# Sorted edge sources placed by one-hot matrix products in PSUM instead of by indirect sends to memory

## The chip, the cores and the metric

The kernel runs on one core of one Trainium2 chip. The metric is the device time of one execution in microseconds; of several executions the median is taken. The profile is one further execution, taken by the hardware profiler.

## The reference

The reference computes one layer of a graph network over 3125 nodes with 256 channels. A normalised copy `xn` of the input goes through two branches whose results are added to the input: a message-passing network (103,125 edges sorted by target, each message a gathered node row and 64 edge attributes, summed by target, followed by a small dense network), and four layers of linear attention with a feed-forward part. Then comes a mixture of four experts, whose gates come from a graph attention over 65,536 unsorted edges. This last part matters here:

```python
h = (x_flat @ W_gat).reshape(M, HEADS, NUM_EXPERTS)
...
a_src = (h * att_src).sum(-1)
a_dst = (h * att_dst).sum(-1)
e = jax.nn.leaky_relu(a_src[src] + a_dst[dst], negative_slope=0.2)
e_max = jax.ops.segment_max(e, dst, num_segments=M)
ee = jnp.exp(e - e_max[dst])
denom = jax.ops.segment_sum(ee, dst, num_segments=M)
alpha = ee / (denom[dst] + 1e-16)
msg = h[src] * alpha[:, :, None]
agg = jax.ops.segment_sum(msg, dst, num_segments=M)
```

To sum by target, the kernel sorts the edges by target itself: it needs, for each place in the sorted order, the source node of the edge that belongs there. Edges whose target is past the last of the 3125 nodes do not count.

## The kernel before

Nodes lie in 25 tiles of 128. The program is one stream of Python code that deals instructions to the engines; a scheduler keeps each engine's queue in order. The parts are these.

**Messages.** `gather_chunk` fetches one row per partition for 806 columns by indirect transfers from GpSimd's queue (line 456), and `sum_up` (line 468, VectorE) adds along the columns. The sums are stored in `run_d`.

**Attention and feed-forward.** The loop over `DEPTH` = 4 layers is TensorE's main work. Between its pieces, calls of `pace(us)` and `beside(us)` deal out other work. `clock["now"]` is a planned time; `pace` advances it, and lets columns of the messages, pieces of the node network and sends follow when their planned time has come. `beside` takes jobs from a list: counting (`count_group`), range tables (`ends_tile`), and 64 placement groups (`place_group`).

**Placement.** The 65,536 edges lie as 128 partitions by `TE` = 512 columns. `place_group` handles 8 columns: with one-hot products it finds each edge's rank in the sorted order (`number`). After four groups `laid` turns 32 columns of ranks into addresses `place`: rank r belongs to partition r // tv, column r % tv of the sorted layout, where tv is 400, or 512 when the edges are many.

**Sends.** `send(t)` (line 736) issues one indirect transfer from GpSimd's queue that writes 128 sources, one of 4 bytes per partition, to their addresses in the memory buffer `by_dst`; 512 of them in all. They begin when the last message column is summed, one per 1.38 us of the planned clock, and no sooner than their place is known. `by_dst` is first filled with a node `NONE` that stands for "no edge"; its row of the table carries a score of -1e30. `sorted_edges` loads the sorted sources `si` back once all sends have landed (line 881).

**Node network.** `message_nodes` starts when the messages are done. `fetch` (line 534) gathers the sums of two tiles by indirect transfers into `aggr` (three buffers), `pair` (lines 539 to 608) runs the small dense network on them in some fifteen pieces. A fetch stands in GpSimd's queue behind the sends that were issued before it.

**Edges.** After the last layer's feed-forward, `finish` (lines 780 to 816) adds the branches, computes the 24 numbers of each node, writes them to the table `tab_d` and to the target positions `tgt_d`. Then 400 indirect gathers by the columns of `si` (line 1064) bring the table's rows, `edge_chunk` runs the softmax along them, and the four experts are computed beside. The last part joins partitions, gates and writes out.

Other lines that the text names: line 643 `one_hot`, line 686 `ohT` (VectorE's comparisons of the placement), lines 695, 722 and 723 its scan and reduction, lines 706 to 720 its products, lines 1011 and 1024 the two products of the feed-forward, line 1021 its 16-bit bias product of 512 columns, line 544 the two-scalar comparison `goes_on`, line 1056 the first row that the edge stage gathers.

Of the kernel before, what the change touches and what calls it, by code (L numbers as in the profile page):

```python
# [48 lines left out]
FEW = 400  # L49
NONE = NT * P - 1  # L50
FF2 = 512
# [6 lines left out]
def kernel(ctx: ExitStack, tc: tile.TileContext, a: dict, out: bass.AP):  # L58
# [131 lines left out]
    tab = state.tile([P, NT, ROW + 1], F32, name="tab")  # L190
    tab_d = dram.tile([NP, ROW], F32, name="tab_d")
    gx_d = dram.tile([NP, D], F32, name="gx_d")
# [120 lines left out]

    pairs0 = so.tile([P, TE], I32, name="pairs0", tag="pairs")
    lo = so.tile([P, TE], F16, name="lo")
    hi = so.tile([P, TE], F16, name="hi")
    row_h = dram.tile([TE // GC, GC * P], F16, name="row_h")
    with tc.tile_pool(name="tmp", bufs=1) as tmp:
# [16 lines left out]
        V.tensor_copy(lo, d)  # L335
        V.tensor_scalar(pairs0, e_src, float(N - 1), None, op0=ALU.min)
    bins = const.tile([P, P, GC], F16, name="bins")
    G.iota(bins, pattern=[[1, P], [0, GC]], base=0, channel_multiplier=0, allow_small_or_imprecise_dtypes=True)
# [59 lines left out]
    def ends_sum():  # L398
# [3 lines left out]
        nc.sync.dma_start(f0[0:P - 1, 1:2], f0[1:P, 0:1])  # L402
        V.tensor_scalar(d0, f0[:, 0:1], 0.0, float(N - 1), op0=ALU.max, op1=ALU.min)
        G.iota(first_t, pattern=[[P, NT]], base=0, channel_multiplier=0, allow_small_or_imprecise_dtypes=True)
# [45 lines left out]
    def gather_chunk():  # L450
        t0 = STARTS[len(chunks)]
        k = min(KM, TM - t0)
        m = mg.tile([P, KM, DM], F32, name="m_run", bufs=3)
        attributes(m, t0, k)
        for t in range(k):
            last_gather[0] = G.indirect_dma_start(  # L456
                out=m[:, t, :D], out_offset=None, in_=xn_d,
                in_offset=bass.IndirectOffsetOnAxis(ap=src_i[:, t0 + t:t0 + t + 1], axis=0))
        chunks.append(m)
# [18 lines left out]

    last_gather = [None]
    for _ in range(3):  # L480
# [6 lines left out]

    pieces = []

    def piece():  # L490
# [4 lines left out]
    def pace(us):  # L495
# [13 lines left out]
        while (clock["columns"] == TM and clock["sent"] < clock["placed"]  # L509
               and FIRST + COLUMN * (TM + NT + clock["sent"] - 32) <= clock["now"]):  # L510
            send(clock["sent"])
            clock["sent"] += 1


    def message_nodes():
        mi_open.close()
        pw = early.enter_context(tc.tile_pool(name="pw", bufs=1))
        wk2 = early.enter_context(tc.tile_pool(name="wk2", bufs=1))
# [12 lines left out]
        def fetch(c):  # L531
            agg = wk2.tile([P, 2, DM], F32, name="aggr", bufs=3)
            for i, t in enumerate(c):
                last_gather[0] = G.indirect_dma_start(  # L534
                    out=agg[:, i, :], out_offset=None, in_=run_d,
                    in_offset=bass.IndirectOffsetOnAxis(ap=sum_i[:, t:t + 1], axis=0))
            fetched[c[0]] = agg

        def pair(c):
            agg = fetched[c[0]]  # L540
            k, n0, w = len(c), c[0] * P, len(c) * P
            for i, t in enumerate(c):
                goes_on = wk2.tile([P, P], F32, name="goes_on")
                V.tensor_scalar(goes_on, ids, last_t[:, t:t + 1], cont, op0=ALU.is_equal, op1=ALU.mult)
                ps = pg.tile([P, DM], F32, name="ps_g")
                T.matmul(ps, goes_on, last_m, start=True, stop=True)
                V.scalar_tensor_tensor(agg[:, i, :], agg[:, i, :], has_m[:, t:t + 1], ps, op0=ALU.mult, op1=ALU.add)
                yield False
            xr = wk2.tile([P, 2, D], F32, name="xr", bufs=2)
            nc.sync.dma_start(xr[:, :k, :], xn_d[n0:n0 + w, :].rearrange("(c p) d -> p c d", p=P))  # L550
            h0 = wk2.tile([P, 2, D], F32, name="h0", bufs=2)
            cmv = small.tile([P, 4, 2], F32, name="cmv")
# [43 lines left out]
            yield False  # L596
            xin = wk2.tile([P, 2, D], F32, name="xin")
            if c[-1] < NT - 1:
# [9 lines left out]
            nc.sync.dma_start(gx_d[n0:n0 + w, :].rearrange("(c p) d -> p c d", p=P), h0[:, :k, :])  # L608
            if c[0] + 6 < NT:
                fetch(PAIRS[c[0] // 2 + 3])  # L610

        for c in PAIRS[:3]:
            fetch(c)
        pieces.extend(pair(c) for c in PAIRS)

    place = so.tile([P, TE], I32, name="place")
    tv = state.tile([P, 1], F32, name="tv")
    many_i = state.tile([P, 1], I32, name="many_i")
    tv_less, tv_inv, tv_gap = (state.tile([P, 1], F32, name=f"tv_{k}") for k in range(3))

    def laid(dst, r):

# [5 lines left out]
        V.tensor_scalar(a, rem, tv, None, op0=ALU.is_ge)  # L628
        V.scalar_tensor_tensor(a, rem, 0.0, a, op0=ALU.is_lt, op1=ALU.subtract)
        V.tensor_tensor(a, q0, a, op=ALU.subtract)  # L630
        V.tensor_scalar(a, a, float(P), tv_gap, op0=ALU.min, op1=ALU.mult)
        V.tensor_tensor(dst, a, r, op=ALU.add)
    by_dst = dram.tile([2 * E2, 1], I32, name="by_dst")
    by_p = by_dst[:E2, :].rearrange("(p t) o -> p (t o)", t=TE)
    nothing = so.tile([P, TE], I32, name="nothing", tag="hr", bufs=2)
    V.memset(nothing, NONE)
    nc.sync.dma_start(by_p, nothing)
    start_d = dram.tile([P, LO], F32, name="start_d")
# [40 lines left out]
    def place_group(t):  # L679
# [31 lines left out]
        if late:  # L711
# [12 lines left out]
            if (t + GC) % SG == 0:  # L724
                laid(place[:, t + GC - SG:t + GC], number[t // SG % 2])
                clock["placed"] = t + GC
# [5 lines left out]

    def send(t):

        with tc.issue_after(last_gather[0].ins):
            i = G.indirect_dma_start(out=by_dst, out_offset=bass.IndirectOffsetOnAxis(ap=place[:, t:t + 1], axis=0),  # L736
                                     in_=pairs0[:, t:t + 1], in_offset=None)
        tc.declare_no_dep(i.ins, group="by_dst", reason="each place is written once")
        tc.add_to_no_dep_group("by_dst", i.ins)

# [39 lines left out]
    def finish(c):  # L780
# [22 lines left out]
        for i in range(2):  # L803
# [4 lines left out]
                            prod[:, :k, :].rearrange("p t (h e) -> p t h e", h=H4), AX.X, ALU.add)  # L808
        if c[-1] == NT - 1:
            V.tensor_scalar(tab[:, NT - 1, HG:HG + H4], tab[:, NT - 1, HG:HG + H4], no_node, None, op0=ALU.add)  # L810
        nc.sync.dma_start(tab_d[n0:n0 + w, :].rearrange("(c p) f -> p c f", p=P), tab[:, c[0]:c[-1] + 1, :ROW])

# [20 lines left out]
    for p0 in range(0, P, 32):  # L833
        nc.sync.dma_start(by_edge[p0:p0 + 32, FEW:, :].rearrange("p t f -> p (t f)").rearrange("p (a b) -> p a b", b=128),
                          zeros[p0:p0 + 32, :, :128].to_broadcast([32, (TE - FEW) * ROW // 128, 128]))
    no_node = state.tile([P, 1], F32, name="no_node")
    V.tensor_scalar(no_node, bin_p, LAST - 0.5, -BIG, op0=ALU.is_ge, op1=ALU.mult)
    V.memset(tab[:, :, ROW:], 1.0)
# [4 lines left out]
    def edge_ranges():  # L843
# [30 lines left out]
        V.tensor_tensor(start_i, start, away, op=ALU.add)  # L874

    edges = {}

    def sorted_edges():

        si = so.tile([P, TE], I32, name="si", tag="oh_hi", bufs=2)  # L880
        tc.keep_in_program_order(nc.sync.dma_start(si, by_p))
        edges.update(si=si)

# [155 lines left out]
    while clock["sent"] < TE:  # L1039
        pace(COLUMN)  # L1040
    sorted_edges()
    early.close()
# [15 lines left out]
    tgt_p = tgt_d[:E2, :].rearrange("(p t) h -> p t h", t=TE)  # L1058
    si = edges["si"]

# [339 lines left out]
```

## Time and profile before

| what | us |
|---|---|
| median of 3 runs (2829.52 to 2834.2) | 2831.46 |
| the profiled execution | 3944.21 |
| its span, first to last instruction | 3942.5 |
| TensorE busy with products | 2327.2 |
| GpSimd busy | 1782.9 |
| VectorE busy | 1440.1 |
| ScalarE busy | 991.9 |
| 806 message gathers on GpSimd, 996 ns each | 802.5 |
| 512 sends on GpSimd, 969 ns each | 495.9 |
| 400 edge gathers on GpSimd, 954 ns each | 381.4 |

The mean granted TensorE clock in it is 0.765. The profiled execution is 1113 us longer than the median run. Durations of single instructions are read from it; how long the engines stand idle between them is not the same in the other runs. A row of a group gives its line, engine, operation, tiles, shape and count, then busy us and the mean ns of one, then the idle time ahead of it and what ended it ("issue": nothing that the profile shows; "remote": another engine that it does not name). PE is TensorE, PEld its weight loads, DVE VectorE, ACT ScalarE, POOL GpSimd, SP the engine that issues the plain transfers.

### The profile page before, as it was taken

The page shows a single profiled execution, that of the slowest core. Times are in us where ns is not written, and L with a number is a line of the kernel's source. Part 1 is how long each engine was busy: PE and PEld are TensorE (multiplying, and loading weights), DVE is VectorE, ACT ScalarE, POOL GpSimd, SP SyncE. Part 2 cuts the span into 40 slices and gives each one's busy share as a digit, 9 for nine tenths or more (in the row PEclk, how much of TensorE's full clock was granted, in tenths as well). Part 3 has the DMA queues.
Part 4 walks back from the last instruction along what each step waited for, and adds up shares of the span by engine and source line. Part 5 has one row for each costly group of instructions (what it writes and reads, how often), then busy time and mean ns, then how long its engine had stood idle before and what let it go on. Part 6 is the DMA issues. An engine that isn't in the chain of part 4 may idle for free. (4 is left out here: it accounts for less than half of the span.)

```text
span 3942.5 us, 33476 instructions
## 1 busy us (share of the span) xinstructions
PE 2327.2 (59%) x11139; PEld 1603.3 (41%) x11139; DVE 1440.1 (37%) x4221; ACT 991.9 (25%) x1721; POOL 1782.9 (45%) x1843
## 2 busy tenths in 40 slices
PE   1756466566488765834563556448268746657471
PEld 1544343445255552523352445336245523334241
DVE  4645354464534544312232333324201112121227
ACT  2312123241122411211221332214123312122121
POOL 3446544454635546365435333430630355554634
PEclk9877687788699977966776777768578867777675
DMA  8446555664645646400001101001000111110101
GB/s 245 151 143 220 178 158 150 188 213 142 207 150 188 227 131 199 145 18 17 26 25 28 49 20 35 18 11 32 16 7 14 22 15 30 12 30 15 26 14 35
DMA packets 282448, 350.07 MB, mean 89 GB/s; under 512 B 180015, under 2 KB 229686, under 8 KB 269462
## 3 DMA queue, kind: packets, MB, share of 16 engines
q1 hardware_dynamic: 211558, 232.39, 18.4%
q0 software_dynamic: 70704, 115.42, 11.2%
q8 instruction: 90, 1.47, 0.2%
q14 instruction: 96, 0.79, 0.1%
HBM read 193.09 MB, written 154.56 MB: 88 GB/s over the span
## 5 line engine op out<-in xcount | busy, mean ns | idle before, releaser
L456 POOL DMA_INDIRECT m_run<-xn_d,src_i x806 | 802.5, 996 | 828.1 <-issue 230.1
L736 POOL DMA_INDIRECT by_dst<-pairs,place x512 | 495.9, 969 | 329.1 <-DVE near L657 161.7
L1064 POOL DMA_INDIRECT rows_c<-tab_d,si x400 | 381.4, 954 | 300.1 <-DVE rows_c L1120 181.2
L468 DVE SCALAR_TENSOR_TENSOR m_run<-m_run,stay 128x320 f32<-128x320 f32 x805 | 439.6, 546 | 98.4 <-DMA m_run<-xn_d,src_i 50.9
L1011 PE MATMUL ps_a<-hT,w 128*128 128x512 f32 (+1 forms) x896 | 405.4, 609 | 80.6 <-ACT hT L164 44.6
L1024 PE MATMUL ps_a<-w,gT 128*128 128x256 f32 x1600 | 380.9, 390 | 58.5 <-issue 57.8
L1024 PEld LDWEIGHTS ps_a<-w,gT 128*128 128x128 f32 x1600 | 310.3, 195 | 122.2 <-issue 80.3
L1152 PE MATMUL ps_a<-hT,we 128*128 128x512 f32 (+1 forms) x448 | 233.5, 654 | 150.5 <-issue 98.6
L1011 PEld LDWEIGHTS ps_a<-hT,w 128*128 128x128 f32 x896 | 177.0, 214 | 283.2 <-issue 178.8
L1163 PE MATMUL ps_t<-we,hf 128*128 128x256 f32 x800 | 201.3, 404 | 83.3 <-issue 61.5
L1027 DVE TENSOR_TENSOR xm<-ps_a,xm 128x512 f32<-128x512 f32 (+1 forms) x52 | 34.9, 670 | 522.8 <-remote 266.5
L1152 PEld LDWEIGHTS ps_a<-hT,we 128*128 128x128 f32 x448 | 92.5, 219 | 305.4 <-issue 241.6
L534 POOL DMA_INDIRECT aggr<-run_d,sum_i x25 | 24.6, 983 | 414.2 <-PE ps_t L557 387.2
L1163 PEld LDWEIGHTS ps_t<-we,hf 128*128 128x128 f32 x800 | 159.9, 203 | 127.8 <-issue 80.6
L1014 ACT ACTIVATE gT<-ps_a,b 128x512 f32<-128x512 f32 (+1 forms) x224 | 142.8, 641 | 239.7 <-PE ps_a L1011 157.5
L581 PE MATMUL ps_a<-gh,gw 128*128 128x256 f32 (+1 forms) x312 | 99.1, 464 | 165.1 <-issue 99.2
L709 ACT ACTIVATE earlier<-ps_t 128x512 f16<-128x512 f32 x128 | 71.8, 594 | 397.0 <-PE ps_t L708 179.1
L695 DVE TENSOR_TENSOR_SCAN run<-goes,ps_g 128x288 f16<-128x288 f16 x64 | 48.1, 751 | 322.6 <-remote 184.0
L994 PE MATMUL ps_a<-co,qT 128*128 128x256 f32 x400 | 123.1, 459 | 72.2 <-ACT qT L953 38.1
L581 PEld LDWEIGHTS ps_a<-gh,gw 128*128 128x128 f32 x312 | 67.8, 235 | 187.3 <-issue 107.7
L971 PE MATMUL ps_g<-vk 128*128 128x128 f32 x400 | 80.0, 330 | 101.7 <-ACT vk L969 60.3
L159 PE MATMUL ps_t<-ident,hn 128*128 128x128 f32 x450 | 90.5, 335 | 69.2 <-ACT hn L122 28.2
(375 smaller groups left out, 3803.5 us busy)
## 6 DMA issues: line engine op xcount, KB each, us to landing
run_d<-m_run SPq DMA_DIRECT2D x100, 1280.0 KB
m_run<-in_edge_attr_dram SPq DMA_DIRECT2D x95, 256.0 KB
hr<-row_h SPq DMA_DIRECT2D x64, 256.0 KB
m_run<-xn_d,src_i POOLq DMA_INDIRECT x806
w<-in_L_mix_W_dram SPq DMA_DIRECT2D x8, 1024.0 KB
by_dst<-pairs,place POOLq DMA_INDIRECT x512
rows_c<-tab_d,si POOLq DMA_INDIRECT x400
run_d<-rows_c SPq DMA_DIRECT2D x16, 300.0 KB
```

The costliest lines, as they stand in the source:

```text
L159: T.transpose(ps[:, i * P:(i + 1) * P], src[:, c * P:(c + 1) * P], ident)
L456: last_gather[0] = G.indirect_dma_start(out=m[:, t, :D], out_offset=None, in_=xn_d, in_offset=bass.IndirectOffsetOnAxis(ap=src_i[:, t0 + t ...
L468: add = V.scalar_tensor_tensor(m[:, t, :], before_m, stay[:, c:c + 1], m[:, t, :], op0=ALU.mult, op1=ALU.add)
L581: T.matmul(ps[:, :w], gw[i][:, kc, m * P:(m + 1) * P], h[:, kc, :w], start=kc == 0, stop=kc == 1)
L736: i = G.indirect_dma_start(out=by_dst, out_offset=bass.IndirectOffsetOnAxis(ap=place[:, t:t + 1], axis=0), in_=pairs0[:, t:t + 1], in_offs ...
L994: T.matmul(ps[:, i, :], qT[:, m, i * P:(i + 1) * P], co[:, m, :], start=m == 0, stop=m == 1)
L1011: T.matmul(ps[:, :n1 - n0], w1[:, kc, f * P:(f + 1) * P], hT[:, kc, n0:n1], start=kc == 0, stop=kc == 1)
L1014: S.activation(gf[:, :n1 - n0], ps[:, :n1 - n0], AF.Gelu, bias=b1[:, f:f + 1])
L1024: T.matmul(ps[:, i, :], gT[f][:, (i0 + i) * P:(i0 + i + 1) * P], w2[:, f, :], start=False, stop=f == FF // P - 1, skip_group_check=True)
L1064: G.indirect_dma_start(out=rows_c[:, t - COLS[j], :], out_offset=None, in_=tab_d, in_offset=bass.IndirectOffsetOnAxis(ap=si[:, t:t + 1], a ...
L1152: T.matmul(ps[:, :w], we1[:, kc, f * P:(f + 1) * P], hT[:, kc, c[0] * P:c[0] * P + w], start=kc == 0, stop=kc == 1)
L1163: T.matmul(ps[:, i, :], hh[f][:, (i0 + i) * P:(i0 + i + 1) * P], we2[:, f, :], start=False, stop=f == FF2 // P - 1, skip_group_check=True)
```

## The change

The sends, the buffer `by_dst`, its first fill and its load are gone. A bank of PSUM, `by_target` (128 by 512, f32), takes their place. For each of the 512 columns of edges, VectorE makes two one-hot matrices in f16: `to_p` (128 edges by 128 partitions: in which partition the edge belongs, four columns in one instruction) and `to_t` (128 edges by 512 columns: in which column, times the edge's source). TensorE multiplies them and adds to the bank, 512 products in all. `spread(t)` does two columns at a call, and issues their products at the next call. At the end one VectorE instruction adds `NONE` and writes `si`.

Since an empty place must read zero, sources are kept as their distance from `NONE`, which is now 2048, in the middle of the table; the table gets one row more, and sources from 2048 on are moved by one. `laid` is split: `divided` gives quotient and remainder, which `place_group` writes to `part_h` (the memory of `hi`) and `col`. To make room, the node network has two `aggr` buffers for three, fetches two pairs ahead for three, has one `xr` and one `h0` for two, and shares buffers for `goes_on` and `xin`. The planned clock lets a column be spread each 0.9 us and adds 0.22 us for each.

```diff
-NONE = NT * P - 1
+NONE = SRC // 2
...
-    pairs0 = so.tile([P, TE], I32, name="pairs0", tag="pairs")
+    pairs0 = so.tile([P, TE], F32, name="pairs0", tag="pairs")
...
         V.tensor_scalar(pairs0, e_src, float(N - 1), None, op0=ALU.min)
+        past = e.bitcast(F32)
+        V.tensor_scalar(past, pairs0, NONE - 0.5, float(-NONE), op0=ALU.is_ge, op1=ALU.add)
+        V.tensor_tensor(pairs0, pairs0, past, op=ALU.add)
...
-               and FIRST + COLUMN * (TM + NT + clock["sent"] - 32) <= clock["now"]):
-            send(clock["sent"])
-            clock["sent"] += 1
+               and FIRST + COLUMN * (TM + 6) + 0.9 * clock["sent"] <= clock["now"]):
+            spread(clock["sent"])
+            clock["sent"] += SC
+            clock["now"] += 0.22 * SC
...
-            agg = wk2.tile([P, 2, DM], F32, name="aggr", bufs=3)
+            agg = wk2.tile([P, 2, DM], F32, name="aggr", bufs=2)
...
-            xr = wk2.tile([P, 2, D], F32, name="xr", bufs=2)
+            xr = wk2.tile([P, 2, D], F32, name="xr")
...
-            h0 = wk2.tile([P, 2, D], F32, name="h0", bufs=2)
+            h0 = wk2.tile([P, 2, D], F32, name="h0")
...
-            if c[0] + 6 < NT:
-                fetch(PAIRS[c[0] // 2 + 3])
+            if c[0] + 4 < NT:
+                fetch(PAIRS[c[0] // 2 + 2])
...
-    nothing = so.tile([P, TE], I32, name="nothing", tag="hr", bufs=2)
-    V.memset(nothing, NONE)
-    nc.sync.dma_start(by_p, nothing)
...
-                laid(place[:, t + GC - SG:t + GC], number[t // SG % 2])
+                q0, rem, a = divided(number[t // SG % 2])
+                V.tensor_tensor(part_h[:, t + GC - SG:t + GC], q0, a, op=ALU.subtract)
+                V.scalar_tensor_tensor(col[:, t + GC - SG:t + GC], a, tv, rem, op0=ALU.mult, op1=ALU.add)
...
-    def send(t):
-
-        with tc.issue_after(last_gather[0].ins):
-            i = G.indirect_dma_start(out=by_dst, out_offset=bass.IndirectOffsetOnAxis(ap=place[:, t:t + 1], axis=0),
-                                     in_=pairs0[:, t:t + 1], in_offset=None)
+    SC = 2
+    spread_of = []
+    by_target = []
+
+    def spread(t):
+
+        sp = sp_open[0]
+        if not by_target:
+            by_target.append(px.tile([P, TE], F32, name="by_target", tag="sums_ps"))
+            by_target.extend((sp.tile([P, P], F16, name="ids_h"), sp.tile([P, TE], F16, name="cols_h")))
+            V.tensor_copy(by_target[1], ids)
+            G.iota(by_target[2], pattern=[[1, TE]], base=0, channel_multiplier=0, allow_small_or_imprecise_dtypes=True)
+        if t < TE:
+            if t % 4 == 0:
+                to_p = sp.tile([P, 4, P], F16, name="to_p", bufs=2)
+                V.tensor_tensor(to_p, by_target[1].rearrange("p (o e) -> p o e", o=1).to_broadcast([P, 4, P]),
+                                part_h[:, t:t + 4].rearrange("p (t o) -> p t o", o=1).to_broadcast([P, 4, P]), op=ALU.is_equal)
+            else:
+                to_p = spread_of[-1][1]
+            to_t = sp.tile([P, SC, TE], F16, name="to_t", bufs=3)
+            for i in range(SC):
+                V.tensor_scalar(to_t[:, i, :], by_target[2], col[:, t + i:t + i + 1], pairs0[:, t + i:t + i + 1],
+                                op0=ALU.is_equal, op1=ALU.mult)
+            spread_of.append((t, to_p, to_t))
+        if t == TE or len(spread_of) > 1:
+            t, to_p, to_t = spread_of.pop(0)
+            for i in range(SC):
+                T.matmul(by_target[0], to_p[:, t % 4 + i, :], to_t[:, i, :], start=t + i == 0, stop=t + i == TE - 1)
...
-        nc.sync.dma_start(tab_d[n0:n0 + w, :].rearrange("(c p) f -> p c f", p=P), tab[:, c[0]:c[-1] + 1, :ROW])
+        r0 = n0 + (n0 >= NONE)
+        nc.sync.dma_start(tab_d[r0:r0 + w, :].rearrange("(c p) f -> p c f", p=P), tab[:, c[0]:c[-1] + 1, :ROW])
...
     while clock["sent"] < TE:
         pace(COLUMN)
-    sorted_edges()
+    spread(TE)
+    si = so.tile([P, TE], I32, name="si", tag="oh_hi", bufs=2)
+    V.tensor_scalar(si, by_target[0], float(NONE), None, op0=ALU.add)
```

## The prediction

> **What bounds the kernel now.** I read four views in this order: busy time by stage, the waits of one stage, what touches `by_dst`, and the rows that price the new instructions. The stages are cut where GpSimd (POOL) changes its work. Busy time by stage; columns are window, length, busy us and count of PE, PEld, DVE, ACT, POOL, then granted clock, DMA share and GB/s:
>
> ```profile
> 0.00:1676.00 1676.00, 1061.82 (x4882) 736.02 (x4883) 816.37 (x2065) 443.50 (x771) 820.74 (x838) 0.82 0.57 179
> 1676.00:2888.00 1212.00, 616.31 (x4201) 464.46 (x4200) 373.10 (x1130) 302.96 (x554) 491.82 (x508) 0.71 0.09 24
> 2888.00:3115.00 227.00, 196.72 (x699) 132.64 (x699) 35.15 (x127) 80.44 (x129) 37.47 (x39) 0.86 0.04 10
> 3115.00:3832.00 717.00, 436.76 (x1300) 257.57 (x1300) 140.50 (x729) 146.58 (x228) 383.44 (x402) 0.75 0.12 22
> 3832.00:3942.00 110.00, 15.60 (x58) 12.65 (x58) 74.99 (x172) 18.43 (x40) 49.45 (x57) 0.50 0.12 35
> ```
>
> Stage 1 gathers the message rows, stage 2 holds nearly all of the 512 sends, stage 3 is the rest of the last feed-forward, stage 4 the edge gathers beside the experts, stage 5 the tail. In stage 2 no engine is busy for much over half the time. Two neighbouring windows of stage 2 say why, the first without and the second with sends:
>
> ```profile
> 2610.00:2760.00 150.00, 120.27 (x611) 90.02 (x612) 73.16 (x214) 62.84 (x111) 0.00 (x0) 0.84 0.09 27
> 2765.00:2888.00 123.00, 27.01 (x294) 22.16 (x293) 22.18 (x79) 11.88 (x23) 78.62 (x81) 0.53 0.04 7
> ```
>
> Without sends TensorE is busy 120.27/150 = 80%, with them 22%. So in this execution a run of sends slows all engines. Whether it does so without the profiler decides the case. The profiled execution took 3944.21 us (span 3942.5, 1.7 us around it), the median run 2831.46: 1113 us of the profiled time are not in the runs that count.
>
> I try to place those 1113 us. Undisturbed, I take TensorE at 80% busy and clock 0.84. Stage 2 then needs 616.31 x 0.71/0.84 / 0.80 = 651 us, which is 561 less; stage 1 needs 1061.82 x 0.82/0.84 / 0.80 = 1296, 380 less; stage 4 is bound by its 400 gathers at 0.954 + 0.30 us (row L1064 and its issue gap), 502 us, plus a first and a last chunk, say 540, 177 less. Stages 3 and 5 stay. Together 1118 us less, 2824 us: near the median. So by this estimate the median run holds almost none of the slowing, and stage 2 takes about 650 us in it, with TensorE as its fullest engine. The weak point is the split: stage 1 could be as short as its 806 gathers at 0.996 + 0.30, 1045 us, and then up to 250 us of slowing could be left in stage 2.
>
> Do sends hold anything by an ordinary wait? The view of what touches `by_dst`, and the waits of stage 2 (who waited <- for whom: us, times, longest):
>
> ```profile
> L736 POOL DMA_INDIRECT by_dst<-pairs,place x512: 957/962/1700, 1665.2 to 2911.0; - x171
> who waited for it (us, times):
>   POOL first_row L1056: 2.7, 1
> ```
>
> ```profile
> POOL aggr L534 <- PE ps_t L557: 387.2, 10, 53.8
> POOL by_dst L736 <- DVE near L657: 161.7, 1, 161.7
> POOL by_dst L736 <- issue: 148.3, 487, 0.3
> ```
>
> Only the load of the sorted list waited for the sends, 2.7 us. POOL itself waited for TensorE to free a node buffer (387.2 us) and for VectorE's places (161.7 us). The last send starts at 2911.0, 204 us ahead of the end of stage 3. The sends are not on the path by any wait.
>
> [...]
>
> ```profile
> L643 DVE TENSOR_TENSOR oh_hi<-bins,hi 128x1024 f16<-128x1024 f16 x128 | 86.9, 682 | 87.5 <-PE sums_ps L653 57.6 <-remote 23.6 <-issue 5.6
> L686 DVE TENSOR_SCALAR ohT<-hr,bin_p 128x1024 f16<-128x1024 f16 x64 | 31.0, 485 | 118.4 <-remote 94.8 <-DMA hr<-row_h 18.2 <-PE ps_g L720 3.5
> L544 DVE TENSOR_SCALAR goes_on<-ids,last_t,cont 128x128 f32<-128x128 f32 x25 | 8.6, 344 | 1.3 <-issue 1.3
> ```
>
> [...] a 16-bit 512-column product being followed 0.22 us later:
>
> ```profile
> 2955.66 0.38 PE L1021 MATMUL ps_a<-b_parts,ones_b 65*128 65x512 bf16 x1
> 2955.88 1.46 PE L1024 MATMUL ps_a<-w,gT 128*128 128x256 f32 x6
> ```
>
> [...]
>
> **The change, part by part.**
> *Removed from POOL:* 512 sends (0.969 + 0.30 us, 650 us of its queue), on the path 0 by the waits above. The cover is POOL's own slack; what then is late next is TensorE, which already was. The fill of `by_dst` and the load of `si` leave SP's queue: -3 us (the 2.7 us wait). A conversion of 512 columns out of PSUM takes its place on DVE, under 1 us, and the gathers wait for it; the last product stands well before the last `finish`, so it is hidden.
> *Added to PE:* 512 products of 512 columns with a weight load each. 512 x 0.22 = 113 us of the queue; a 128x128 f16 weight load has a mean of 106 ns (row L706 of PEld) and fits under the product before it. They stand in stage 2 and the start of stage 3, between feed-forward, node and placement products. Lower bound: the 20% of gaps take their share, 113 x 0.8 = 90. Upper: they run at the stage's clock and leave the gaps, 113/0.84/0.80 = 168. I take 113, the two corrections cancelling.
> *Added to DVE:* [...] 280 us in all. DVE's load in stage 2 goes from 373 to about 653 us, in a stage of 651 + 113 = 764 us: 85%. In-order behind these stand the norms, the placement scans and the feed-forward adds, on which PE waits. Bounds: 0 if they fall in DVE's gaps (391 us of them), 100 if over a third shows. I take 25.
> *Node pairs:* buffers shrink (`aggr` 3 to 2; `xr`, `h0` 2 to 1). Fetches no longer stand behind 42 sends (55 us at 1.27), so two buffers are enough; the load of `xr` can now hold SP's queue, with placement loads behind it, until the pair before has read it. 13 pairs x 0 to 2 us; I take 5.
> *Moved table row, sentinel, two-way division of the place:* as many small DVE operations as before, within a microsecond or two; 0.
> *Slowing by sends that is left in the median run:* nothing to 250 us. I take 35 gained, since the sum above leaves almost nothing.
>
> Sum: 113 + 25 + 5 - 3 - 35 = +105 us. In the profiled execution the same work is added, but the slowing of stage 2 (up to 561 us) goes with the sends; there I expect some 3500 to 3700 us instead of 3944. For the median run: 2831 + 105 = 2936 us.
>
> **Rivals.**
> *Sends slowed the engines without the profiler too.* Mechanism: a run of over some 20 sends in stage 2 starves PE, ACT and DVE, as in the 2765 window. For it: 22% against 80%. Against: 1113 us of idle time are gone without the profiler, and from 2888 to 2912 us PE was busy all 24 us beside 19 indirect transfers (15 sends, 4 others). It decides from the point at which more than 140 us (113 + 25 + 5 - 3) of slowing are left in stage 2; in the middle between that and 250, 195 us: 2831 + 140 - 195 = 2776 us, faster.
> *VectorE becomes the bound.* If [...] the chains queue behind it, stage 2 takes what DVE needs at the 80% that PE reaches: (373 + 280)/0.80 = 816[...]. Taking 830 to 850: 180 to 200 us on top of 651, 3020 us. [...]
> *It cancels.* A slowing of about 140 us is left: 2831 us.
>
> **Chances.** 0.2% (about 6 us) is what a measurement can tell from no change. Forecast, 2840 to 2985: 0.54. DVE-bound, 2985 to 3080: 0.17. Faster, 2690 to 2825: 0.25. Cancelled: 0.04. Slower 0.71, same 0.04, faster 0.25. The range 2765 to 3030 leaves out the lower half of the faster case and a third of the DVE case, under 0.2 together; the likeliest case alone is 2840 to 2985.
>
> **What would show it.** In the profile after: `to_t` near 0.41 and `to_p` 0.42 to 0.68 us; the products 0.22 us apart; POOL empty but for fetches in stage 2; PE at 80% or more there, DVE near 85% of it or below; a span below 3942 although the runs are slower. Wrong if the runs fall below 2831: then sends were a cost without the profiler. Wrong in size if DVE waits lead stage 2.

## The result, and the profile after

The changed kernel takes 2948.86 us (median of four runs, 2942.34 to 2951.53) where the kernel before takes 2832.83 (2829.52 to 2835.95): ratio 1.0406, 95% interval 1.0385 to 1.0428. It is 116 us slower. Its profiled execution takes the same 2948.86 us, span 2947.1.

One thing must be known to read the numbers: runs of one session agree within about 1%, but whole sessions differ, on the same chip too, so that the kernel before takes 2830 to 2838 us in some (here called short: its timing, and the last of the four sessions below) and 3934 to 4005 in others (long: the first three below, and by its length of 3944 us its profile too), and ratios are therefore taken within a session.

Busy time by stage of the changed kernel, cut as in the prediction (message gathers; placement with the new work; the rest of the last feed-forward; edges; tail). Columns: window, length, then busy us and count of PE, PEld, DVE, ACT, POOL, then granted clock, DMA share, GB/s:

```profile
0.00:1205.00 1205.00, 953.62 (x4710) 677.67 (x4711) 804.35 (x2038) 437.60 (x763) 814.80 (x823) 0.90 0.78 243
1205.00:2039.00 834.00, 740.18 (x4900) 519.35 (x4899) 619.92 (x1786) 312.06 (x566) 26.15 (x27) 0.92 0.14 42
2039.00:2260.00 221.00, 189.17 (x688) 129.54 (x687) 36.10 (x129) 76.44 (x124) 24.90 (x26) 0.86 0.06 14
2260.00:2832.00 572.00, 384.64 (x1299) 245.32 (x1297) 124.79 (x665) 148.14 (x226) 383.20 (x401) 0.83 0.16 24
2832.00:2947.00 115.00, 14.23 (x58) 12.12 (x58) 86.16 (x232) 19.01 (x42) 49.82 (x58) 0.50 0.13 37
```

In stage 2 POOL runs only 27 short instructions (26 us), TensorE is busy 740/834 = 89%, VectorE 620/834 = 74%. The second and third line together, 1055 us, are the part of the program that the change touches. The new instructions of the same profile; a row ends with busy us, mean ns, then the idle time of the engine ahead of them and who ended it:

```profile
L766 DVE TENSOR_SCALAR to_t<-cols_h,col,pairs 128x512 f16<-128x512 f16 x512 | 178.8, 405 | 0.8 <-PE by_target L772 0.6
L772 PE MATMUL by_target<-to_t,to_p 128*128 128x512 f16 x512 | 160.0, 390 | 22.3 <-DVE to_t L766 21.9
L760 DVE TENSOR_TENSOR to_p<-ids_h,hi 128x512 f16<-128x512 f16 x128 | 87.1, 681 | 5.8 <-PE by_target L772 5.7
```

`to_t` takes 405 ns for an expected 0.41 us, `to_p` 681 ns, the upper end of an expected 0.42 to 0.68 us. These prices, and with them the 280 us of new VectorE work in the forecast, were the author's estimates; no row of before shows them for these shapes. VectorE waits for nobody over these (0.8 and 5.8 us), and TensorE waits 22 us for `to_t`. So far the profile looks as the forecast had it: products in TensorE's queue, VectorE hidden. The experiments say otherwise.

### The profile page after: what moved, and what is told of

It reads as the page before. It is cut to its first block, busy times and chain, and to the rows that moved or that the text cites. A ratio compares the mean times of both kernels' runs of the same rounds, so it can differ in the third digit from the quotient of the medians.

```text
span 2947.1 us, 34625 instructions
## 1 busy us (share of the span) xinstructions
PE 2281.8 (77%) x11651; PEld 1584.0 (54%) x11651; DVE 1671.3 (57%) x4850; ACT 993.3 (34%) x1721; POOL 1298.9 (44%) x1332
## 5 line engine op out<-in xcount | busy, mean ns | idle before, releaser
L1037 PE MATMUL ps_a<-hT,w 128*128 128x512 f32 (+1 forms) x896 | 389.9, 588 | 40.4 <-DVE xm L1053 32.6
L1050 PE MATMUL ps_a<-w,gT 128*128 128x256 f32 x1600 | 363.1, 382 | 0.0
L1179 PE MATMUL ps_a<-hT,we 128*128 128x512 f32 (+1 forms) x448 | 198.9, 597 | 56.1 <-ACT hf L1181 50.8
L846 POOL DMA_INDIRECT tgt_d<-tab,start_i x25 | 24.0, 959 | 397.6 <-DVE tab L840 382.5
L1190 PE MATMUL ps_t<-we,hf 128*128 128x256 f32 x800 | 185.9, 386 | 15.2 <-ACT hf L1181 15.2
L766 DVE TENSOR_SCALAR to_t<-cols_h,col,pairs 128x512 f16<-128x512 f16 x512 | 178.8, 405 | 0.8 <-PE by_target L772 0.6
L772 PE MATMUL by_target<-to_t,to_p 128*128 128x512 f16 x512 | 160.0, 390 | 22.3 <-DVE to_t L766 21.9
L1020 PE MATMUL ps_a<-co,qT 128*128 128x256 f32 x400 | 109.8, 420 | 42.8 <-DVE q L967 34.0
L122 ACT ACTIVATE hn<-xm,rstd 128x256 f32<-128x256 f32 x225 | 118.4, 594 | 18.5 <-DVE rstd L118 17.9
L1020 PEld LDWEIGHTS ps_a<-co,qT 128*128 128x128 f32 x400 | 80.3, 209 | 61.9 <-ACT qT L979 22.4
```

Source lines behind the costliest of these rows:

```text
L122: S.activation(dst, src, AF.Identity, bias=r[:, 1, i:i + 1], scale=r[:, 0, i:i + 1])
L766: V.tensor_scalar(to_t[:, i, :], by_target[2], col[:, t + i:t + i + 1], pairs0[:, t + i:t + i + 1], op0=ALU.is_equal, op1=ALU.mult)
L772: T.matmul(by_target[0], to_p[:, t % 4 + i, :], to_t[:, i, :], start=t + i == 0, stop=t + i == TE - 1)
L1020: T.matmul(ps[:, i, :], qT[:, m, i * P:(i + 1) * P], co[:, m, :], start=m == 0, stop=m == 1)
L1037: T.matmul(ps[:, :n1 - n0], w1[:, kc, f * P:(f + 1) * P], hT[:, kc, n0:n1], start=kc == 0, stop=kc == 1)
L1050: T.matmul(ps[:, i, :], gT[f][:, (i0 + i) * P:(i0 + i + 1) * P], w2[:, f, :], start=False, stop=f == FF // P - 1, skip_group_check=True)
```

## The experiments

The measure that carries over from session to session is the stretch from the start of the last message gather to the start of the first edge gather (stages 2 and 3): without sends hardly a transfer by indices runs in it (25 fetches of the node network and 25 stores of `finish`). The changed kernel needs 1055.9 us for it in its first profile and 1055.5 in its second. No kernel without sends was profiled in both kinds of session. That its stretch carries over is read from the waits: with sends, in the long session of "before, once more", VectorE stands 510 us of the stretch in waits ended by "remote"; without sends it is at most 4 us in the profiles of long sessions and none in those of short ones. All results, with the median of the kernel before in the same session:

| kernel | before in its session | its median | ratio, 95% interval | the stretch, us |
|---|---|---|---|---|
| before, once more | 3948 | 3970 | one run | 1486 |
| before, no sends | 3948 | 3349 | 0.848 (0.845 to 0.851) | 885 |
| before, small buffers | 3948 | 3930 | 0.995 (0.992 to 0.997) | 1464 |
| after, neither one-hots nor products | 3948 | 3359 | 0.851 (0.848 to 0.854) | 893 |
| after, short products | 3991 | 3552 | 0.892 (0.889 to 0.895) | 1062 |
| after, products but no one-hots | 3991 | 3425 | 0.859 (0.856 to 0.862) | 934 |
| after, planned clock not advanced | 3991 | 3536 | 0.887 (0.884 to 0.890) | 1048 |
| before, no sends, second time | 3981 | 3370 | 0.845 (0.841 to 0.849) | 883 |
| after, `to_p` columns innermost | 3981 | 3521 | 0.885 (0.879 to 0.890) | 1038 |
| after, `to_p` columns innermost, half of `to_t` on GpSimd | 3981 | 3790 | 0.951 (0.947 to 0.955) | 1299 |
| after, one-hots but 18 products | 2835 | 2966 | 1.047 (1.045 to 1.049) | 1058 |
| after, once more | 2835 | 2947 | 1.040 (1.038 to 1.041) | 1056 |

**Before, once more.** No edit.

> The kernel before, unchanged, for a second profile. Added-work theory: the slowing of stage 2 was the first profile's own, so a profile can come out near the median of 2832, with the end of the gathers near 1210 us as in the kernel after, and stage 2 about 116 us shorter than in the kernel after. Theory that sends slow the engines: the 2765 window's picture (TensorE at 22% busy beside sends) comes back at a shorter span too.

It took 3970 us, and the timed runs of the same kernel in that session took 3934 to 3967, while the profiled execution of the changed kernel takes exactly its median. So it is not the profiler that stretches an execution. The prediction had put the 1113 us between profile and median down to the profile; what differs, as far as the runs show, is the session.

**Before without its sends.**

```diff
     def send(t):
-        with tc.issue_after(last_gather[0].ins):
-            i = G.indirect_dma_start(out=by_dst, ...)
+        return
...
-        tc.keep_in_program_order(nc.sync.dma_start(si, by_p))
+        V.tensor_copy(si, pairs0)
```

> The kernel before without the 512 sends; the unsorted sources stand in for the sorted ones, so the gates are of the wrong edges. Added-work theory: sends are hidden, within 6 us of before (2827 to 2838), at most 35 us faster. Theory that sends cost time without the profiler: 100 us or more faster (below 2735).

The median falls by 599 us (3948 to 3349), and the stretch by 601 (1486 to 885), so all of it lies there. Stages 2 and 3 of before, once more (busy time by stage, columns as above):

```profile
1653.00:2911.00 1258.00, 642.68 (x4380) 484.20 (x4379) 383.55 (x1158) 310.14 (x564) 509.38 (x528) 0.72 0.10 28
2911.00:3138.00 227.00, 194.67 (x693) 132.11 (x692) 35.78 (x129) 77.74 (x126) 34.89 (x37) 0.84 0.05 14
```

The same two without sends:

```profile
1632.00:2283.00 651.00, 587.17 (x4368) 459.21 (x4367) 382.27 (x1158) 304.93 (x559) 23.96 (x25) 0.92 0.17 52
2283.00:2516.00 233.00, 201.05 (x705) 134.68 (x704) 35.92 (x131) 81.34 (x130) 25.21 (x27) 0.84 0.06 14
```

VectorE and ScalarE have the same work in stage 2 of both (383.55 and 382.27; 310.14 and 304.93), TensorE nearly the same count of products (4380 and 4368; it is busy 643 and 587 us, at a clock of 0.72 and 0.92), and the length falls from 1258 to 651 us. Stage 3 stays about the same (227 and 233 us). Here the sends were a heavy cost. The undisturbed stage 2 of 651 us is the length that the prediction had worked out, but by luck: its sum has 521 us of TensorE (616.31 x 0.71/0.84) at 80% busy, the run 587 us at 90%.

**Before with the changed kernel's buffers.**

```diff
-            agg = wk2.tile([P, 2, DM], F32, name="aggr", bufs=3)
+            agg = wk2.tile([P, 2, DM], F32, name="aggr", bufs=2)
...
-            xr = wk2.tile([P, 2, D], F32, name="xr", bufs=2)
-            h0 = wk2.tile([P, 2, D], F32, name="h0", bufs=2)
+            xr = wk2.tile([P, 2, D], F32, name="xr")
+            h0 = wk2.tile([P, 2, D], F32, name="h0")
...
-            if c[0] + 6 < NT:
-                fetch(PAIRS[c[0] // 2 + 3])
+            if c[0] + 4 < NT:
+                fetch(PAIRS[c[0] // 2 + 2])
```

`goes_on` and `xin` share buffers as in the changed kernel too.

> The kernel before with the node network's buffers and the two-pair fetch of the kernel after, sends kept. Added-work theory: +0 to +10 us. Theory that the lost buffers make the change slow: +60 us or more. With sends ahead of the fetches the smaller lead could cost more here than in the kernel after, so a small number excludes that theory, a large one does not prove it.

18 us less than before, 0.5%. Fewer buffers cost nothing here.

**The changed kernel with neither one-hots nor products.** It leaves the sorting of the sources out; only the buffers, the division of the place, the moved table row and the advance of the planned clock are left of the change.

```diff
     def spread(t):
+        return
...
-    V.tensor_scalar(si, by_target[0], float(NONE), None, op0=ALU.add)
+    V.tensor_scalar(si, pairs0, float(NONE), None, op0=ALU.add)
```

> The kernel after with neither one-hots nor products; unsorted sources stand in for the sorted ones. Buffers, planned clock and everything else as after. Added-work theory: at or near before less what sends cost, 2800 to 2845. Theory that buffers or the planned clock make the change slow: near the kernel after, 2920 to 2949.

The stretch takes 893 us, 8 more than before without sends. That is all that buffers, division and plan cost, the prediction's "+5". Its stage 2:

```profile
1634.00:2294.00 660.00, 594.51 (x4372) 463.36 (x4370) 380.92 (x1146) 306.23 (x561) 25.42 (x26) 0.92 0.17 52
```

What takes the stretch from 893 us (long session) to 1056 (short) must then be one-hots and products: 163 us. The next runs divide it.

**The changed kernel with short products.** Each product but the first has 64 columns in place of 512, so most of the sorting is left out.

```diff
-                T.matmul(by_target[0], to_p[:, t % 4 + i, :], to_t[:, i, :], ...)
+                n = TE if t + i == 0 else 64
+                T.matmul(by_target[0][:, :n], to_p[:, t % 4 + i, :], to_t[:, i, :n], ...)
```

> The kernel after with the products cut to 64 of 512 columns (the first one keeps 512); the other columns of the sorted list stay at the first product's values, so most edges gather the wrong row. One-hots on VectorE are all made. Theory that the products' time on TensorE is the cost: [...] some 65 to 90 us faster than after, about 2870. Theory that VectorE's one-hots are the cost: within 20 us of after (2930 to 2949).

The stretch takes 1062 us, none less than 1056. Seven eighths of each product are gone and nothing is gained. Its stage 2:

```profile
1656.00:2498.00 842.00, 702.93 (x4906) 520.48 (x4905) 619.48 (x1785) 312.85 (x568) 25.27 (x27) 0.83 0.13 41
```

TensorE is busy 37 us less than in the changed kernel (703 for 740), at a clock of 0.83 for 0.92, and VectorE as long as there. A product has a median of 193 ns for 379. If busy time goes inversely with the granted clock, which is an estimate, the 703 us would be 703 x 0.83/0.92 = 634 at the changed kernel's clock: the lower clock takes back part of the time that was cut, and what is left of it shortens nothing.

**The changed kernel with products but no one-hots.** The products read constant zero tiles, so the sorting is left out.

```diff
-                to_p = sp.tile([P, 4, P], F16, name="to_p", bufs=2)
-                V.tensor_tensor(to_p, ...)
+                to_p = by_target[3]
...
-            to_t = sp.tile([P, SC, TE], F16, name="to_t", bufs=3)
-            for i in range(SC):
-                V.tensor_scalar(to_t[:, i, :], ...)
+            to_t = by_target[4]
```

> The kernel after with all 512 products, of constant zero matrices in place of the one-hots: 512 to_t and 128 to_p fewer on VectorE; unsorted sources stand in for the sorted ones. Theory of the products: 20 to 40 us faster than after, about 2920. Theory of VectorE's one-hots: 70 us or more faster, 2850 to 2880.

The stretch takes 934 us: all 512 products cost 41 us over the 893, in place of the 113 of their queue. Its stage 2:

```profile
1668.00:2369.00 701.00, 676.63 (x4886) 498.81 (x4884) 386.77 (x1149) 306.32 (x560) 24.62 (x27) 0.97 0.16 49
```

Where the rest went can be read off beside the 660 us without products. TensorE's time not busy falls from 660 - 594.51 = 65 us to 701 - 676.63 = 24, so 41 us of products went into gaps; and the clock rises from 0.92 to 0.97, which on 677 us is, by the estimate that busy time goes inversely with it, another 0.05 x 677 = 34. 41 + 34 + 41 = 116, near the 113 of 512 x 0.22 us. The operands are zeros here; whether the clock rises as far with other data, no run shows.

**The changed kernel without the advance of the planned clock.**

```diff
-            clock["now"] += 0.22 * SC
```

> The kernel after without the 0.22 us that the planned clock adds for each column; the work is the same, its order in the queues differs. Added-work theory: within 15 us of after. Theory that the changed plan (later pieces and sums behind the spreads) makes the change slow: 40 us or more faster.

The stretch takes 1048 us, 8 less than in the changed kernel's own profile from a short session; the plan's share, by that comparison, is about that. This run also serves as the changed kernel in a session where before takes near 3990 us: there the change would make the kernel 11% faster, because there the sends cost 601 us.

**Before without its sends, second time.** The edit is that of the first.

> The kernel before without its 512 sends, once more; it leaves the sorting of the sources out, the edge gathers read the unsorted ones. It prices the sends on a chip where the kernel before takes near 2832 us. Theory (there the sends cost only a little, since the gathers of the first stage and the tail are not slowed either): 55 us less than before, ratio 0.98, about 2777 us, and the stretch from the last message gather to the first edge row takes 885 us as in its first run. Rival (there the sends cost nothing, and the whole difference of the changed kernel is what it adds): within 10 us of before, ratio 1.00. If the chip is one where before takes near 3950 us, ratio 0.85 as in the first run, and only the stretch of 885 us is new.

883 us after 885: the stretch repeats within 2 us. The session was again a long one, so what the sends cost in a short one was not measured by this run.

**`to_p` with its four columns innermost.**

```diff
-                to_p = sp.tile([P, 4, P], F16, name="to_p", bufs=2)
-                V.tensor_tensor(to_p, ... .to_broadcast([P, 4, P]), part_h[...] .to_broadcast([P, 4, P]), op=ALU.is_equal)
+                to_p = sp.tile([P, P, 4], F16, name="to_p", bufs=2)
+                V.tensor_tensor(to_p, bins[:, :, :4], part_h[...] .to_broadcast([P, P, 4]), op=ALU.is_equal)
...
-                T.matmul(by_target[0], to_p[:, t % 4 + i, :], to_t[:, i, :], ...)
+                T.matmul(by_target[0], to_p[:, :, t % 4 + i], to_t[:, i, :], ...)
```

> The changed kernel with to_p laid out with the four columns innermost[...]. Theory (VectorE's one-hots set the added time, about 0.4 us of it for each us of VectorE work): to_p falls from 681 to 420 ns, 33 us less VectorE work, the stretch from the last message gather to the first edge row falls from about 1050 to 1035 us. Rival (the weights of the products are then read with a stride of four elements and load slower, 512 of them): the stretch stays or grows, by up to 50 us. On a chip where before takes near 2832 us that is 2935 us or 2950 to 3000; where before takes near 3950, ratio 0.89 or above.

The rows of the new `to_p` and of its weight loads:

```profile
L760 DVE TENSOR_TENSOR to_p<-bins,hi 128x512 f16<-128x512 f16 x128 | 55.1, 431 | 9.9 <-PE by_target L772 9.7
L772 PEld LDWEIGHTS <-to_p 128*128 128x128 f16 x512 | 57.7, 115 | 67.7 <-issue 32.6 <-DVE to_p L760 13.4 <-DVE to_t L766 2.5
```

`to_p` falls from 681 to 431 ns and 32 us of VectorE's work go; the stretch falls by 18 us, to 1038 (1035 were expected). Weights with a stride of four load in 115 ns, those of the changed kernel in 100, and the rival's 50 us do not come. In the first layout the operand from `part_h` repeats one element along the innermost direction, in this one neither operand does. L643 of before is laid out as this one is and does 1024 elements in 682 ns, about the 681 that the first layout needs for 512. No run tests the repeated element apart from the rest of the layout.

**Half of `to_t` on GpSimd**, `to_p` with its columns innermost as well:

```diff
-                V.tensor_scalar(to_t[:, i, :], ...)
+                (G if i else V).tensor_scalar(to_t[:, i, :], ...)
```

> The same, and every second to_t is made by GpSimd, which is nearly idle in that stage. Theory (VectorE's time is what the one-hots cost): VectorE loses 104 + 33 us of work, and if GpSimd makes one in about 1 us, the stretch from the last message gather to the first edge row falls from about 1050 to 990 us. Rival A (the products and their place in TensorE's queue cost the time): the stretch stays at 1050. Rival B ([...] GpSimd needs over 2 us for one): the stretch grows past 1100 us. On a chip where before takes near 2832 us: 2885, 2945 or over 3000 us; where before takes near 3950: ratio 0.87, 0.885 or over 0.90.

The stretch takes 1299 us, 261 more than with the new `to_p` alone. The rows of `to_t` on both engines, and of the products:

```profile
L766 POOL TENSOR_SCALAR to_t<-cols_h,col,pairs 128x512 f16<-128x512 f16 x256 | 540.3, 2120 | 237.0 <-DVE col L737 231.3 <-PE by_target L772 5.2 <-DVE b_parts L149 0.2
L772 PE MATMUL by_target<-to_t,to_p 128*128 128x512 f16 x512 | 220.8, 510 | 194.7 <-POOL to_t L766 193.5 <-DVE to_t L766 0.9
L766 DVE TENSOR_SCALAR to_t<-cols_h,col,pairs 128x512 f16<-128x512 f16 x256 | 115.7, 461 | 95.7 <-PE by_target L772 95.5
```

One comparison takes GpSimd 2120 ns, over five times VectorE's 405. Each pair of columns then takes over 2 us, TensorE stands 193.5 us in front of GpSimd's tiles (2.5 us at most each time), and VectorE in turn 95.5 us for its buffers: rival B of that run, with its "over 2 us for one". In each partition GpSimd needs 2120/512 = 4.1 ns per element here, VectorE 405/512 = 0.8. That VectorE is dear does not make any idle engine a cheaper one.

**The changed kernel with its one-hots but 18 of the 512 products.** Most of the sorting is left out.

```diff
-            for i in range(SC):
-                T.matmul(by_target[0], to_p[:, t % 4 + i, :], to_t[:, i, :], ...)
+            if t % 64 == 0 or t + SC == TE:
+                for i in range(SC):
+                    T.matmul(by_target[0], to_p[:, t % 4 + i, :], to_t[:, i, :], ...)
```

> The changed kernel with all its one-hots made as before, but only 18 of the 512 products issued; it leaves most of the sorting of the sources out. The stretch from the last message gather to the first edge row is read, 1056 us in the changed kernel, 934 without one-hots and 893 without either. Theory (VectorE's own work is what costs: the one-hots push back norms, scans and adds on which TensorE waits): the stretch stays at 1000 to 1050 us. Rival (the one-hots cost only because the products stand at the head of TensorE's queue and wait there for them; without products nobody waits): it falls to about 900 us. In between, 930 to 990, both have a share. The ratio to the kernel before follows on the kind of chip: where before takes near 3950, 0.88 or 0.85.

The stretch takes 1058 us, as long as with all products, 8 above what the theory allowed and far from the rival's 900. Its median is even 18 us above the changed kernel's; 14 of them lie in the edge stage, whose gathers then mostly fetch the row `NONE` (the stage takes 586 us in place of 572, with its DMA share at 0.56 for 0.16). Its stage 2:

```profile
1206.00:2041.00 835.00, 644.03 (x4401) 488.78 (x4400) 616.05 (x1779) 309.86 (x565) 25.76 (x28) 0.82 0.14 41
```

TensorE is now idle 835 - 644 = 191 us of it, for 65 with neither one-hots nor products. Its busy time rises as well, 644 us for 595 with 18 products more, at a clock of 0.82 for 0.92: up to 50 of the 165 us that the stretch is longer are TensorE's own work, slower. The waits of TensorE in that window (waiting tile <- who let it go: us, times, longest) say for whom it stands idle:

```profile
PE ps_t L718 <- DVE ohT L696: 33.5, 9, 15.1
PE ps_g L701 <- DVE rest L668: 22.6, 8, 13.5
PE ps_a L589 <- DVE gh L592: 22.2, 8, 11.4
PE ps_t L159 <- ACT h L122: 20.3, 6, 11.8
...
PE ps_a L1008 <- DVE cT L1005: 14.3, 1, 14.3
```

With neither one-hots nor products the same waits are

```profile
PE ps_t L979 <- DVE q L973: 15.7, 5, 5.3
PE ps_a L589 <- DVE gh L592: 10.0, 6, 3.0
PE ps_t L159 <- ACT h L122: 7.0, 4, 2.9
PE ps_t L718 <- DVE ohT L696: 4.1, 6, 1.1
```

The placement's `ohT` and `rest`, the node network's `gh`, the norm ahead of `h`, the attention's `cT`: each is an ordinary VectorE instruction (or one of ScalarE behind one) on which TensorE waits, and each comes up to 15 us late when one-hots stand ahead of it in VectorE's queue.

VectorE's queue in the same run, ahead of the longest of these waits, and the end of that wait on TensorE (start, us, engine, line, operation, times in a row, then the idle time ahead of it):

```profile
1971.33 0.68 DVE L760 TENSOR_TENSOR to_p<-ids_h,hi 128x512 f16<-128x512 f16 x1
1971.93 1.37 DVE L766 TENSOR_SCALAR to_t<-cols_h,col,pairs 128x512 f16<-128x512 f16 x4
...
1984.59 0.68 DVE L760 TENSOR_TENSOR to_p<-ids_h,hi 128x512 f16<-128x512 f16 x1
1985.19 1.37 DVE L766 TENSOR_SCALAR to_t<-cols_h,col,pairs 128x512 f16<-128x512 f16 x4
1986.48 0.59 DVE L732 SCALAR_TENSOR_TENSOR own_bin<-ps_g,oh_lo 128x256 f32<-128x256 f32 x1
1986.99 0.20 DVE L708 TENSOR_TENSOR base<-run,near 128x32 f32<-128x32 f16 x1
1987.12 0.47 DVE L696 TENSOR_SCALAR ohT<-hr,bin_p 128x1024 f16<-128x1024 f16 x1
1987.65 0.82 PE L718 MATMUL ps_t<-ohT 128*128 128x128 f16 x6 [15.10 <-DVE ohT L696]
```

From 1971.33 to 1986.48 VectorE makes the one-hots of 32 columns and nothing else, eight `to_p` and 32 `to_t`, and TensorE, which needs the `ohT` behind them, waits 15.10 us. The code says why they come so: places become known for 32 columns at once, and where the planned time of these columns has passed by then, `pace` deals out all 32 in one go, whatever the 0.9 us per column.

The changed kernel has eight such blocks too, of 14.6 to 16.0 us; they hold 122 of the 253 us in which VectorE makes one-hots. There TensorE runs products meanwhile. It is busy 106 of 122 us in these blocks, where with 18 products it is busy 45, and its waits look small:

```profile
PE by_target L772 <- DVE to_t L766: 21.9, 38, 2.0
PE ps_a L589 <- DVE gh L592: 9.7, 6, 3.0
PE ps_g L701 <- DVE rest L668: 6.1, 6, 2.8
PE ps_t L718 <- DVE ohT L696: 4.5, 5, 1.5
```

A kernel that deals a group's columns out evenly was not run. The nearest is the one without the advance of the planned clock: blocks of 10 us or more hold 101 us in it, for 133 in the changed kernel, and its stretch is 8 us shorter. So how much of the cost is the blocks, and how much is VectorE's added work in any order, stays open.

**The changed kernel, once more.** No edit.

> The changed kernel once more. If the chip is one where the kernel before takes near 3950 us: 3535 us, ratio 0.89, since stage 1 and the edge stage are slowed with or without the sends, and the stretch from the last message gather to the first edge row takes 1056 us as in its first profile (theory: without sends in it that stretch is the same on every chip). Rival: it is slowed there too, to 1150 us or more, and the ratio is above 0.91. If it is one where before takes near 2832 us: 2949 us, ratio 1.04.

It came in the same session as the run before it, where before takes 2835 us: 2947 us, ratio 1.040, the stretch 1055.5. For long sessions there is only the run without clock advance (1048 us there), whose stretch was not slowed.

## Why the prediction was right in the total and wrong in its parts

2936 us were forecast, 2949 measured, within the likeliest case's own range (2840 to 2985). That the total came so near is luck. Products were charged 113 us and one-hots 25, 138 together, and they cost 163 together, in quite another way; against that, the relief from the sends was taken as 35 us and is estimated at about 56 below.

- **"Added to PE: I take 113".** Wrong. Without one-hots the products cost 41 us, below the lower bound of 90: they filled gaps, and the granted clock was 0.97 with them for 0.92 without. Beside the one-hots they add nothing on balance: 1058 us with 18 of them, 1056 with 512, since they fill TensorE's waits and the clock of stage 2 is 0.92 with them and 0.82 without. The step charged the queue time of an engine that stood 10% of the stage idle and ran below its full clock, and would have to wait for VectorE besides.
- **"Added to DVE: I take 25", bounds 0 to 100.** Wrong, and the step that failed. One-hots alone cost 1058 - 893 = 165 us, outside the bounds. The cover named was VectorE's gaps, 391 us of them; but in these gaps VectorE mostly waited for an input of its next piece (with neither one-hots nor products, in stage 2: `gh` 86.0 us for ScalarE, `h` 53.3 and `xm` 37.2 us for TensorE), TensorE needs the answer, and when the input comes, a block of one-hots of up to 15 us can stand in front of it. VectorE's busy time in stage 2 rises by 616 - 381 = 235 us and the stretch by 165: 70% of it shows. The author's estimates of single instructions were right (405 ns for 0.41; 681 for 0.42 to 0.68). By count times mean the work is 512 x 0.405 + 128 x 0.681 = 295 us for the 280 taken.
- **The two costs don't add.** 165 and 41 alone, 163 together. They fill the same time: while VectorE is behind, TensorE has room for products.
- **Node pairs, division, plan, "+5".** 8 us measured, 893 against 885; the plan's clock has perhaps another 8 within the 163. The load of `si`, 3 us, can't be told apart; the conversion in its place took 0.68 us (L1069 of the changed kernel).
- **"Slowing by sends that is left: I take 35 gained".** By what is left over, about 56 us: the changed kernel outside its stretch takes 2948.86 - 1055.9 = 1893 us, so the kernel before has 2832.83 - 1893 = 940 for its own, and 885 of that need no sends. This takes the other stages to be equal in both kernels and the stretch without sends to be the same in both kinds of session; stage 1 varied by 36 us among the runs of long sessions (1631 to 1667), so 56 is an estimate to within some 20 us. No profile of before was had from a short session, and the share stays unmeasured there.
- **The sum.** 163 + 8 - 56 = 115 us for a measured 116. It closes because the sends' share is the remainder; what is measured is the +163 and the +8.
- **The rival "VectorE becomes the bound".** It had the mechanism, and the stage: 830 to 850 us were given for stage 2, 834 are measured. Its 3020 us was too high since it left the relief from the sends out (and the rest of the feed-forward takes 221 us for 233 without the change). Its picture, VectorE full, does not hold for the stage (74%) but holds in parts of it: of the 83 slices of 10 us from 1205 us on, VectorE is busy over 90% in 31, and in 7 of 66 with neither one-hots nor products. It is full in stretches, which its mean load does not show, and in these TensorE's work comes late.
- **The rival "sends slow the engines without the profiler too".** In short sessions, where the kernel was timed, the sends' slowing is the 56 us estimated above, below the 140 from which this rival decides; in long ones it is true, the sends cost 601 us and the change wins. The prediction read the difference of 1113 us as the profiler's. It expected "3500 to 3700" for the profile of the changed kernel, which came at 2949 from a short session; in a long one, without the clock advance, it is 3541.

No version here beats the kernel before in a short session: the one with the columns of `to_p` innermost is the shortest of those that sort, 18 us below the changed kernel in the stretch (measured in a long session), while 116 would be needed.

## What to carry to other kernels

Work put on an engine that is half idle was not free here, where a busier engine kept waiting for that engine's answers (one-hots alone cost 165 us, on a VectorE that was 381/660 = 58% busy without them): ask what stands behind each new instruction in its queue, and how many new instructions can come in one row: here it was 15 us of them. Test each half of a change alone, since two costs that fill the same time neither add up nor show by their own waits. Queue time added to the busiest engine was too high a guess here: of 113 us, 41 went into its gaps, and by the estimate above the higher clock made up for 34. And before idle time in a profile is priced, compare the profiled execution with the timed ones: if they lie 39% apart, the profile may be of another regime.

## What the runs showed of the hardware

Sessions in which the kernel takes longer wherever GpSimd issues transfers by indices were not expected. On one and the same chip the kernel before took 3972 to 4005 us in one session and 2830 to 2838 in a later one. The stretches with hardly such a transfer are nearly equal in both kinds (1048 and 1062 us in long sessions for two variants of the changed kernel, 1056 and 1058 in short ones), those with many are not. The edge stage with its 400 gathers takes 692 us in the run without clock advance and 572 in the changed kernel. Stage 1 with its 806 gathers, in the run without clock advance:

```profile
0.00:1658.00 1658.00, 1037.52 (x4711) 717.84 (x4712) 803.63 (x2038) 438.27 (x763) 802.67 (x823) 0.82 0.56 177
```

Against the first line of the changed kernel's stages the same work takes 1658 us for 1205, VectorE's, ScalarE's and GpSimd's busy times being equal within 2% (803.63 and 804.35; 438.27 and 437.60; 802.67 and 814.80), and a gather's median 946 ns in both. So these three engines don't work slower, they stand idle longer; TensorE's busy time is 9% longer at a clock of 0.82 for 0.90. The idle time can be recognised: in the long stage 1 VectorE's waits ended by "remote" come to 285 us and ScalarE's to 373, and TensorE's ended by "issue" to 162, where the short one has none of them. What makes a session long stays open.

In stage 2 the granted clock went with the share of time that TensorE stood idle: 0.97 at 3.5% idle (products, no one-hots), 0.92 at 10% (neither) and 11% (the changed kernel), 0.83 at 17% (short products), 0.82 at 23% (18 products), 0.72 at 49% (before, once more). Which of the two drives the other, these runs do not separate.
